# The edge list of a graph network's third layer: its search moved under the first attention and the neighbours' mean, its counting beside experts three to seven

## The chip, the cores and the metric

The kernel runs on one core of a Trainium2 chip. The metric is the device time of one launch in microseconds (us): the time before is 2432.49 us, the median of three runs (2429.66 to 2437.47). Engines are called as the profile calls them: PE multiplies matrices, DVE, ACT and POOL work on elements, SP issues most transfers.

## What is computed

The model has four layers over a graph of 2,708 nodes with 256 features each. Every layer normalises its input, mixes over the graph and adds, then normalises again, applies a feed-forward part and adds. Only the parts that this change touches are cut out here:

```python
# layer 0, over the graph: attention with weights exp(cosine) where adj > 0
x = x + _L0_gnn_ref(_layernorm(x), adj, ...)
# layer 1, over the graph: mean of the neighbours, projected
x1 = a @ x / deg
return concatenate([x1, x]) @ weight + bias
# layer 1, feed-forward: two of eight experts for each node
h = gelu(xf @ W1[e] + b1[e]);  out = out + w_dense[:, e] * (h @ W2[e] + b2[e])
# layer 2, over the graph: attention with leaky scores, softmax, elu
attention = softmax(where(adj > 0, leaky(wh1 + wh2.T), NEG_BIG));  elu(attention @ wh)
# layer 2, feed-forward: a router that reads a list of 1,048,576 edges
src, dst = edge_index;  e = leaky(a_src[src] + a_dst[dst]);  segment_max, segment_sum over dst
```

The edge list does not depend on any layer's result. Its nodes are drawn from 65,536 numbers and only those with a destination below 2,708 matter, so the kernel first searches the list for the edges that count and then counts them by destination. That work is needed only by the feed-forward part of layer 2.

## The kernel before

The queues of the five engines are ordered ahead of the run by a planner: of the instructions that are ready by its own costs it takes the one that was written earliest. `tc.issue_after(ins)` adds one condition: what is written in its block on the engine of `ins` comes behind `ins` on that engine. Instructions of the block on other engines are not bound by it. Functions that contain `yield` are generators; one `next` writes one step.

**First attention** (`fast_l0_gnn`). The 2,708 targets are cut into six chunks of 512 (the last has 148), the sources into 22 tiles of 128. For each pair of chunk and tile, `scores` loads a tile `aj` of the adjacency (SP, six buffers), multiplies keys and queries (L1791, PE), takes the exponential (L1815, ACT) and masks it (L1816, DVE). Two pairs later, `sums` multiplies the weights with the values (L1842, PE). At a chunk's end `finish` copies the four accumulators (L1862) and finishes the rows.

**Neighbours' mean** (`fast_l1_gnn`). For each of the same chunks in the order 0, 1, 5, 2, 3, 4 and for each tile, SP loads `aj` (ten buffers), ACT checks it (L2470), DVE casts it to `at` (L2495, ten buffers) and PE adds up (L2501). Beside it the router of the experts is computed by another generator, `after`.

**Experts** (`fast_l1_ffn`). For each of eight experts, POOL gathers 768 rows by index (`xe`, L2979), PE turns them (`xt_ps`, L3268) and multiplies them with both weight matrices (`h_ps`, L3282; `y_ps`, L3299), DVE adds the bias and scales (`ys`, L3307 and L3308), POOL adds the rows to `acc` in memory (L3311). `x` is read back from `acc` by `load_x` (L71) after the last expert's additions.

**The edge list** (`Edges`). `search` runs over eight chunks of 128 x 1,024 edges. Each is loaded by two transfers of 512 KB (L2592, L2594), turned into keys by five DVE instructions (L2597 to L2603), and its largest keys are taken out in nine rounds, eight at a time, by MAX8 and MATCH_REPLACE8 (L2608, L2609); a reduction (L2612) checks that nothing is left. `count` has a set-up on DVE (splitting the keys, taking out the rare edges, ranking them, with 32 products on PE, L2732), and then 18 count steps: each compares 32 keys with all node numbers (L2773: `oh` with 4,096 and `ol` with 704 elements to a partition) and adds up 32 products on PE (L2780).

In this version all of the search is written behind the experts: one step (a whole chunk) or more behind the last `ys` of each, by the numbers (1, 1, 2, 1, 2, 1, 3, 2). The third step of expert six is the whole set-up, the other four of experts six and seven are count steps. The other 14 count steps are written in the **second attention** (`fast_gat` with one head), one behind every fifth tile's weights (L3500, DVE; the sums are L3576, PE). The search waits for the router by a scalar, `route.start`, that enters its first instruction.

Of the kernel before, what the change touches and what calls it, by code (L numbers as in the profile page):

```python
# [8 lines left out]
F32 = mybir.dt.float32  # L9
# [1678 lines left out]
def fast_l0_gnn(k, adjT, wqkT, pool_):  # L1688
# [6 lines left out]
    with ExitStack() as ctx:  # L1695
# [88 lines left out]
        def scores(g, j):  # L1784
# [29 lines left out]
            for p, n, r, aj in todo:  # L1814
                nc.scalar.activation(PT[p, :n], s[p, :n], AF.Exp, scale=r)  # L1815
                nc.vector.scalar_tensor_tensor(  # L1816
                    PT[p, :n], aj[p, :n], 0.0, PT[p, :n], ALU.is_gt, ALU.mult
                )
            return PT

        last = {}
# [67 lines left out]
        for i in range(len(todo) + 2):  # L1889
            if i < len(todo):  # L1890
                ahead.append(scores(*todo[i]))
            for _ in range(2 if i < NT else 1):
                next(side, None)
            if i > 1:
# [7 lines left out]
        for _ in side:  # L1902
            pass
# [502 lines left out]
def fast_l1_gnn(k, adjT, weight, bias, order, after):  # L2406
# [6 lines left out]
    with ExitStack() as ctx:  # L2413
# [44 lines left out]
        tmp = ctx.enter_context(tc.tile_pool(name="a1o", bufs=4))  # L2458
# [26 lines left out]
        for i, g in enumerate(order):  # L2485
# [4 lines left out]
            for j in range(NT - 1):  # L2490
# [4 lines left out]
                nc.vector.tensor_copy(at[:, :cs], aj[:, :cs])  # L2495
# [48 lines left out]
            if i < len(order) - 1:  # L2544
                side = after(c0, cs, i, psum)

# [12 lines left out]
class Edges:  # L2559
# [12 lines left out]

    def __init__(self, k, w, pool):
# [9 lines left out]
    def search(self, n):  # L2583

        nc, tc = self.k.nc, self.k.tc
        L = self.L
        with tc.tile_pool(name="et", bufs=2) as tmp:
            ed = self.w["edge_index"].rearrange("s (p c) -> s p c", p=128)
            for c in range(CHEDGE):
# [5 lines left out]
                a = tmp.tile([128, CE], F32, name="a")  # L2595
                key = tmp.tile([128, CE], F32, name="key")
                nc.vector.tensor_scalar(a, si, 0.0, n, ALU.is_lt, ALU.mult)  # L2597
                nc.vector.scalar_tensor_tensor(a, si, 1.0, a, ALU.add, ALU.add)
                nc.vector.tensor_scalar(a, a, 1.0, float(N), ALU.max, ALU.min)
                nc.vector.scalar_tensor_tensor(  # L2600
                    key, di, float(1 << SHIFT), a, ALU.mult, ALU.add
# [3 lines left out]
                )  # L2605
                for r in range(RA):
# [4 lines left out]
                    )  # L2611
                nc.vector.tensor_reduce(self.left[:, c : c + 1], key, AX.X, ALU.max)  # L2612
                yield

    def count(self):
        nc, tc = self.k.nc, self.k.tc
        with tc.tile_pool(name="ep", bufs=1, side="right") as pp, tc.tile_pool(
# [28 lines left out]

            O = pp.tile([128, OA], F32, name="O")
# [25 lines left out]
            nc.vector.tensor_scalar(before, ioi, pc, None, ALU.is_gt)  # L2673
            rp = bank[:, : 5 * OW]
# [49 lines left out]
            for i in range(4):  # L2724
# [5 lines left out]
                )  # L2730
            for c in range(OA):
# [25 lines left out]

            nc.vector.tensor_scalar(hi, hi, 1.0, None, ALU.add)
            nc.vector.scalar_tensor_tensor(
                hi, sr, float(N - 1), hi, ALU.is_equal, ALU.mult  # L2760
            )
            nc.vector.tensor_scalar(hi, hi, -1.0, None, ALU.add)
            hib = pp.tile([128, LW], BF16, name="hib")
            lob = pp.tile([128, LW], BF16, name="lob")
            nc.vector.tensor_copy(hib, hi)
            nc.vector.tensor_copy(lob, lo)
# [92 lines left out]
class Route:  # L2859
# [14 lines left out]
    def __init__(self, k, ctx, w, most):  # L2874
# [13 lines left out]
        self.start = keep.tile([128, 1], F32, name="start")  # L2888
# [322 lines left out]
    def slots(self):  # L3211
# [6 lines left out]
        v.tensor_scalar(self.start, idf[:, 0:1], 0.0, float(N), ALU.mult, ALU.add)  # L3218
# [6 lines left out]
def fast_l1_ffn(k, side, route, rest):  # L3225

# [7 lines left out]
    with ExitStack() as ctx:  # L3234
# [119 lines left out]
        side = iter(side(route.start))  # L3354
        nxt = [one, half(0, 1)]
        run(first)
        for e in range(E):
# [13 lines left out]
            with tc.issue_after(now[-1].last.ins):  # L3371
                for _ in range((1, 1, 2, 1, 2, 1, 3, 2)[e]):
                    next(side)
        k.load_x(lambda r: acc[1 + r.start : 1 + r.stop], lambda ld: wait_for(ld, adds[E - 1]))


def fast_gat(k, adjT, W, a, H, elu, col, side, parts=CHUNKS, after=None):
# [10 lines left out]
    with ExitStack() as ctx:  # L3388
# [173 lines left out]
        for i, (c0, cs) in enumerate(parts):  # L3562
            if H == 1:
# [3 lines left out]
                for j in range(NT - 1):  # L3567
                    PT = weights(c0, cs, j, 0, adjacency(c0, cs, j))
                    if j % 5 == 4:
                        with tc.issue_after(made[0].ins):  # L3570
                            next(side, None)
# [898 lines left out]
def model(tc, I, out):  # L4470
# [4 lines left out]
    with tc.tile_pool(name="flags", bufs=1) as fp:  # L4475
# [4 lines left out]
        with ExitStack() as ctx:  # L4480
            k = Fast(ctx, tc, I["x"], bad, adjT)
            with ExitStack() as c0:
                pooling = Pooling(k, part(I, "L0_ffn_"), c0)
                fast_l0_gnn(k, adjT, I["L0_gnn_WqkT"], pooling)
# [108 lines left out]
```

## Time and profile before

| | |
|---|---|
| median of three runs | 2432.49 us |
| the profiled execution's own time | 2434.38 us |
| its span | 2432.6 us |
| granted clock of PE | 0.953 |
| PE busy | 2263.4 us (93%) |
| DVE busy | 1534.7 us (63%) |
| ACT busy | 666.4 us (27%) |
| POOL busy | 435.0 us (18%) |
| MAX8 and MATCH_REPLACE8, L2608 and L2609 | 72 each, 1225 and 1215 ns |
| count comparisons, L2773 | 18 of 4,466 ns and 18 of 930 ns |

The stages lie in this order in the profiled execution, by the first and last products of each: first attention 31.5 to 362 us, its feed-forward part to 557, projections of the mean to 610, neighbours' mean to 791, experts 797 to 1164.4, projections of the second attention from 1198.5, second attention 1235.1 to 1455.6, then the rest, which the change does not touch.

A row of a timeline gives start, length, engine, line, operation and tiles, and in brackets how long the engine was idle before it and what released it. PE's row of a group of products begins with the first and ends with the last of them. PE products of 32-bit data are recorded twice each.

### The profile page before, as it was taken

To read this page: it belongs to the slowest core of one execution; us is meant where nothing else is said; L and a number is where in the kernel's file an instruction comes from. 1 tells how busy PE (TensorE), PEld (TensorE's weight loads), DVE (VectorE), ACT (ScalarE), POOL (GpSimd) and SP (SyncE) were. 2 spreads that over 40 slices of the span, in tenths; PEclk is the share of its full clock that TensorE was granted. 3 is DMA by queue.
4 is the path that set the end of the run, shared out by engine and by line. 5 is a ranking of instruction groups with operands and counts; after the bars stand their busy time and mean duration, and the time that the engine had idled before them with its cause. 6 is when DMAs were issued, how large, how long until landed. Compare 5 with 4: busy or idle time off the path is not lost. (4 is left out here: it accounts for less than half of the span.)

```text
span 2432.6 us, 31798 instructions
## 1 busy us (share of the span) xinstructions
PE 2263.4 (93%) x11620; PEld 1512.2 (62%) x11620; DVE 1534.7 (63%) x3402; ACT 666.4 (27%) x1347; POOL 435.0 (18%) x496
## 2 busy tenths in 40 slices
PE   7999999988999899999599999999889999968997
PEld 4777765677878667767478877666653333325664
DVE  7544338555445378899779863142579999863544
ACT  6433333214663332231210013232321111111121
POOL 3000003004000333413350002520030000002321
PEclk9999999879999999999799997999899999978999
DMA  4233322200774344423244523000024444315440
GB/s 144 66 99 100 96 57 77 74 1 11 222 217 123 111 128 116 115 51 56 67 132 131 160 72 58 21 1 1 10 71 116 114 113 113 93 44 172 122 128 15
DMA packets 158572, 220.00 MB, mean 90 GB/s; under 512 B 30911, under 2 KB 94115, under 8 KB 158404
## 3 DMA queue, kind: packets, MB, share of 16 engines
q1 hardware_dynamic: 126096, 179.84, 25.4%
q0 software_dynamic: 15488, 24.04, 4.6%
q10 hardware_dynamic: 16820, 13.95, 1.8%
q8 instruction: 96, 1.57, 0.3%
q14 instruction: 72, 0.59, 0.1%
HBM read 193.49 MB, written 24.82 MB: 90 GB/s over the span
## 5 line engine op out<-in xcount | busy, mean ns | idle before, releaser
L3500 DVE SCALAR_TENSOR_TENSOR PT<-Rr,Q,aj 128x512 f32<-128x512 f32 (+3 forms) x630 | 403.2, 702 | 39.3 <-PE acc_ps L3576 26.9
L3651 PE MATMUL acc_ps<-PT,V 128*64 128x512 f32 (+4 forms) x2016 | 328.5, 549 | 0.4 <-ACT Rr L101 0.4
L3651 PEld LDWEIGHTS acc_ps<-PT,V 128*64 128x64 f32 (+1 forms) x2016 | 95.2, 122 | 210.2 <-issue 154.6
L1842 PE MATMUL acc_ps<-fa,PT 128*128 128x257 f32 x882 | 214.1, 382 | 0.5 <-DVE PT L1816 0.5
L1842 PEld LDWEIGHTS acc_ps<-fa,PT 128*128 128x128 f32 x882 | 164.6, 190 | 63.7 <-issue 41.0
L3576 PE MATMUL acc_ps<-V,PT 128*128 128x257 f32 x882 | 200.5, 385 | 2.6 <-DVE hp L3606 1.5
L3576 PEld LDWEIGHTS acc_ps<-V,PT 128*128 128x128 f32 x882 | 165.9, 191 | 31.4 <-issue 3.3
L3282 PE MATMUL h_ps<-xT,w1t 128*128 128x384 f32 x512 | 174.4, 499 | 4.5 <-ACT xT L3273 4.5
L3299 PE MATMUL y_ps<-w2t,hT 128*128 128x256 f32 x768 | 171.0, 382 | 2.7 <-DVE ys L3307 2.7
L1816 DVE SCALAR_TENSOR_TENSOR PT<-aj,PT 128x512 f32<-128x512 int32 (+1 forms) x126 | 79.8, 640 | 147.4 <-ACT PT L1815 147.3
L3299 PEld LDWEIGHTS y_ps<-w2t,hT 128*128 128x128 f32 x768 | 146.2, 192 | 25.3 <-DVE ys L3307 3.9
L2501 PE MATMUL acc_ps<-V,at 128*128 128x257 bf16 x1323 | 158.0, 278 | 3.6 <-DVE at L2495 3.6
L2501 PEld LDWEIGHTS <-at 128*128 128x128 bf16 x1323 | 130.0, 100 | 26.4 <-issue 4.9
L3282 PEld LDWEIGHTS h_ps<-xT,w1t 128*128 128x128 f32 x512 | 97.7, 194 | 73.3 <-ACT xT L3273 8.1
L1815 ACT ACTIVATE PT<-s_ps,rq 128x512 f32<-128x512 f32 (+1 forms) x126 | 79.3, 636 | 168.3 <-PE s_ps L1791 167.1
L3311 POOL DMA_INDIRECT acc<-ys,ids x48 | 86.2, 1796 | 216.3 <-DVE ys L3308 175.2
L1791 PE MATMUL s_ps<-KT,QT 128*128 128x512 f32 (+1 forms) x252 | 116.4, 546 | 1.1 <-POOL KT L1770 0.9
L3997 PE MATMUL y_ps<-w2t,hT 128*128 128x256 f32 (+1 forms) x528 | 117.2, 379 | 0.0
L3984 PE MATMUL h_ps<-fT,w1t 128*128 128x512 f32 (+1 forms) x288 | 115.6, 551 | 0.5 <-ACT hT L3991 0.4
L4420 PE MATMUL y_ps<-w2t,hT 128*128 128x256 f32 (+1 forms) x512 | 112.8, 379 | 0.0
L3997 PEld LDWEIGHTS y_ps<-w2t,hT 128*128 128x128 f32 (+1 forms) x528 | 97.7, 186 | 22.3 <-issue 8.2
L3289 ACT ACTIVATE hT<-h_ps,b1t 128x384 f32<-128x384 f32 x128 | 74.2, 580 | 113.4 <-PE h_ps L3282 112.7
(744 smaller groups left out, 3359.9 us busy)
## 6 DMA issues: line engine op xcount, KB each, us to landing
aj<-in_adjT SPq DMA_DIRECT2D x399, 256.0 KB
w1t<-in_L_ffn_W SPq DMA_DIRECT2D x8, 1024.0 KB
w2t<-in_L_ffn_W SPq DMA_DIRECT2D x8, 1024.0 KB
w1t<-in_L_ffn_w SPq DMA_DIRECT2D x8, 1024.0 KB
w2t<-in_L_ffn_w SPq DMA_DIRECT2D x8, 1024.0 KB
aj<-in_adjT SPq DMA_DIRECT2D x63, 74.0 KB
fd<-fa ACTq DMA_DIRECT2D x9, 512.0 KB
aj<-in_adjT SPq DMA_DIRECT2D x21, 202.0 KB
```

Source lines behind the costliest of these rows:

```text
L1791: nc.tensor.matmul(s[:, :cs], lhsT=QT[:, j * 128 : j * 128 + 128], rhs=KT[:, c0 : c0 + cs], start=True, stop=True,)
L1842: nc.tensor.matmul(ac, lhsT=PT[:, o : o + n], rhs=fa[:, j, :], start=j == 0, stop=False)
L2501: nc.tensor.matmul(ac[:, c:], lhsT=at[:, o : o + n], rhs=V[:, j, r], start=j == 0 and q == 0, stop=False, skip_group_check=True,)
L3282: nc.tensor.matmul(hp, lhsT=w1t[:, kk, m * 128 : (m + 1) * 128], rhs=self.xT[:, kk, :], start=(kk == 0), stop=(kk == 1),)
L3299: nc.tensor.matmul(y, lhsT=self.hT[:, m, i * 128 : (i + 1) * 128], rhs=w2t[:, m, :], start=(m == 0), stop=(m == M - 1),)
L3311: add = nc.gpsimd.indirect_dma_start(out=acc, out_offset=bass.IndirectOffsetOnAxis(ap=self.ids[:, i : i + 1], axis=0), in_=ys, in_offset=None,
L3500: return nc.vector.scalar_tensor_tensor(PT, R, Q, aj, ALU.max, ALU.mult)
L3576: nc.tensor.matmul(ac[:n], lhsT=PT[:, o : o + n], rhs=V[:, j, 0, :], start=(j == 0), stop=False,)
L3651: nc.tensor.matmul(w.pop("out"), **w)
L3984: nc.tensor.matmul(o[:, :cs], lhsT=w1t[:, kk, m * 128 : (m + 1) * 128], rhs=fT[:, kk, c0 : c0 + cs], start=(kk == 0), stop=(kk == 1),)
L3997: nc.tensor.matmul(y[:n], lhsT=hT[:, m, o : o + n], rhs=w2t[:, m, :], start=(m == 0), stop=(m == M - 1),)
L4420: nc.tensor.matmul(y[:n], lhsT=hT[:, m, o : o + n], rhs=w2t[:, m, :], start=(m == 0), stop=(m == M - 1),)
```

## The change

The list's tiles are made ahead of the first attention, and the search becomes a generator of small steps: one that loads, then eleven for each chunk (keys in two, each round of MAX8 and MATCH_REPLACE8 one; the reduction belongs to the last). The loads of the next chunk are written as soon as the keys of this one are made, into the same single buffers. Three searches share the eight chunks:

- chunks 0 to 3 in the first attention, one step behind the mask of every second pair, from the second target chunk on;
- chunks 4 and 5 in the neighbours' mean, one step behind every fourth cast of the first five chunks;
- chunks 6 and 7 behind experts 0 and 1 (12 and 11 steps). The set-up is cut into three steps, the first two behind expert 2, and the 18 count steps are spread behind experts 3 to 6 (four steps of which one is set-up, then 5, 5, 5), with one last copy behind expert 7.

The second attention gets no steps. The search no longer takes `route.start`, and the scratch pool of the mean has two buffers instead of four.

```diff
 def fast_l0_gnn(k, adjT, wqkT, pool_, other):
...
-                nc.vector.scalar_tensor_tensor(
+                made[0] = nc.vector.scalar_tensor_tensor(
                     PT[p, :n], aj[p, :n], 0.0, PT[p, :n], ALU.is_gt, ALU.mult
                 )
...
+            if i >= NT and i % 2:
+                with tc.issue_after(made[0].ins):
+                    next(other, None)
...
 def fast_l1_gnn(k, adjT, weight, bias, order, after, other):
...
-        tmp = ctx.enter_context(tc.tile_pool(name="a1o", bufs=4))
+        tmp = ctx.enter_context(tc.tile_pool(name="a1o", bufs=2))
...
-                nc.vector.tensor_copy(at[:, :cs], aj[:, :cs])
+                made = nc.vector.tensor_copy(at[:, :cs], aj[:, :cs])
+                if i < 5 and j % 4 == 1:
+                    with tc.issue_after(made.ins):
+                        next(other, None)
...
-    def search(self, n):
+    def search(self, chunks, side):
-        with tc.tile_pool(name="et", bufs=2) as tmp:
+        with tc.tile_pool(name="et", bufs=1, side=side) as tmp:
...
+            key = tmp.tile([128, CE], F32, name="key")
+            si, di = load(chunks[0])
+            yield
+            for c in chunks:
+                nc.vector.tensor_scalar(key, si, 0.0, float(N), ALU.is_lt, ALU.mult)
+                nc.vector.scalar_tensor_tensor(key, si, 1.0, key, ALU.add, ALU.add)
+                nc.vector.tensor_scalar(key, key, 1.0, float(N), ALU.max, ALU.min)
+                yield
                 nc.vector.scalar_tensor_tensor(
-                    key, di, float(1 << SHIFT), a, ALU.mult, ALU.add
+                    key, di, float(1 << SHIFT), key, ALU.mult, ALU.add
                 )
                 nc.vector.scalar_tensor_tensor(
                     key, key, float((N << SHIFT) + 1), key, ALU.is_lt, ALU.mult
                 )
+                if c != chunks[-1]:
+                    si, di = load(c + 1)
+                yield
                 for r in range(RA):
                     v = L[:, (c * RA + r) * 8 : (c * RA + r + 1) * 8]
                     nc.vector.max(v, key)
                     nc.vector.match_replace(
                         out=key, in_to_replace=v, in_values=key, imm_value=-1.0
                     )
+                    if r < RA - 1:
+                        yield
                 nc.vector.tensor_reduce(self.left[:, c : c + 1], key, AX.X, ALU.max)
                 yield
...
-        v.tensor_scalar(self.start, idf[:, 0:1], 0.0, float(N), ALU.mult, ALU.add)
...
+        steps_of = (12, 11, 2, 4, 5, 5, 5, 1)
...
             with tc.issue_after(now[-1].last.ins):
-                for _ in range((1, 1, 2, 1, 2, 1, 3, 2)[e]):
+                for _ in range(steps_of[e]):
                     next(side)
...
                 for j in range(NT - 1):
                     PT = weights(c0, cs, j, 0, adjacency(c0, cs, j))
-                    if j % 5 == 4:
-                        with tc.issue_after(made[0].ins):
-                            next(side, None)
...
+                    fast_l0_gnn(
+                        k, adjT, I["L0_gnn_WqkT"], pooling, edges.search(range(4), "right")
+                    )
...
+                        edges.search(range(4, 6), "left"),
...
+                    search = edges.search(range(6, CHEDGE), "right")
+                    fast_l1_ffn(k, chain(search, edges.count()), route, rest)
+                fast_gat(k, adjT, I["L2_gnn_W"], I["L2_gnn_a"], 1, True, 2, iter(()))
```

In `count`, two `yield`s are added in the set-up (ahead of the products that rank, and ahead of the 32 products L2732), and the nine lines that make `hib` and `lob`, the operands of L2773, move from the end of the set-up to its beginning.

## The prediction

> **What bounds the kernel now.** I read the busy times by stage first, then PE's timeline of the three stages that the edge list's work leaves or enters, then DVE, POOL and SP where a stage ends. Columns of the windows: length, then busy time and instructions of PE, PEld, DVE, ACT, POOL, then clock and DMA.
>
> ```profile
> 95.00:340.00 245.00, 245.00 (x1039) 177.42 (x1038) 96.60 (x254) 82.83 (x128) 0.00 (x0) 1.00 0.34 91
> 610.00:776.00 166.00, 162.37 (x1446) 134.53 (x1447) 77.34 (x262) 102.28 (x279) 1.23 (x3) 0.97 0.66 202
> 797.00:1164.40 367.40, 356.31 (x1412) 258.80 (x1413) 292.95 (x468) 92.49 (x167) 135.34 (x96) 0.98 0.37 94
> 1164.40:1198.50 34.10, 5.51 (x160) 5.30 (x159) 22.81 (x51) 2.32 (x4) 11.81 (x11) 0.55 0.43 109
> 1235.10:1455.60 220.50, 216.34 (x1415) 180.87 (x1415) 189.81 (x286) 12.76 (x28) 26.69 (x27) 0.99 0.44 129
> ```
>
> These are the first attention, the neighbours' mean, the experts, the gap behind them, and the attention behind (the second). PE sets the pace in all but the gap. DVE has room in the first two (39% and 47%), little in the experts (80%) and the second attention (86%).
>
> ```profile
> 1235.12 8.04 PE L3576 MATMUL acc_ps<-V,PT 128*128 128x257 f32 x36 [0.64 <-DMA aj<-in_adjT]
> 1244.80 0.95 PE L2780 MATMUL edge_ps<-ol,oh 128*128 128x22 bf16 x32 [1.64 <-DVE ol L2773]
> ...
> 1282.39 6.31 PE L3576 MATMUL acc_ps<-V,PT 128*128 128x257 f32 x28 [1.17 <-DVE hp L3606]
> ...
> 1323.84 6.31 PE L3576 MATMUL acc_ps<-V,PT 128*128 128x257 f32 x28 [0.38 <-DVE hp L3606]
> ...
> 1365.23 6.60 PE L3576 MATMUL acc_ps<-V,PT 128*128 128x257 f32 x28 [0.33 <-DVE rd L3602]
> ...
> 1403.68 37.05 PE L3576 MATMUL acc_ps<-V,PT 128*128 128x257 f32 x168
> 1441.30 2.00 PE L3576 MATMUL acc_ps<-V,PT 128*128 128x257 f32 x8
> ```
>
> Second attention, one line near each chunk's start: chunks with 4, 4, 4, 2 and 0 count steps take 47.3, 41.5, 41.4, 38.4 and 37.6 us.
>
> ```profile
> 896.10 0.82 PE L3268 MATMUL xt_ps<-ident,xe 128*128 128x128 f32 x6
> ...
> 939.50 0.82 PE L3268 MATMUL xt_ps<-ident,xe 128*128 128x128 f32 x6
> ...
> 1027.38 0.82 PE L3268 MATMUL xt_ps<-ident,xe 128*128 128x128 f32 x6
> ...
> 1086.22 32.98 PE L3299 MATMUL y_ps<-w2t,hT 128*128 128x256 f32 x144 [2.41 <-DVE ys L3307]
> 1119.03 0.82 PE L3268 MATMUL xt_ps<-ident,xe 128*128 128x128 f32 x6
> ...
> 1154.63 9.74 PE L3299 MATMUL y_ps<-w2t,hT 128*128 128x256 f32 x44
> ```
>
> Experts: expert 2 takes 43.4 us, undisturbed. Experts 3 and 4 take 87.9, 5 and 6 take 91.7, and expert 7, up to its last product at 1164.4, takes 45.3.
>
> ```profile
> 1157.37 5.42 POOL L3311 DMA_INDIRECT acc<-ys,ids  x1 [0.30 <-DVE rt L2697]
> ...
> 1171.09 4.43 DVE L2773 TENSOR_TENSOR oh<-io,lob 128x4096 bf16<-128x4096 bf16 x1
> 1171.55 5.39 POOL L3311 DMA_INDIRECT acc<-ys,ids  x1 [0.30 <-issue]
> ...
> 1179.16 0.93 SPq L71 DMA_DIRECT2D x<-acc  x2
> ```
>
> The gap: the expert's rows wait on DVE for the set-up, the last addition starts 7.2 us after the last product, is stretched by a count comparison from its usual 1.59 to 5.39 us, and only then are rows read back. PE waits until 1198.5.
>
> **The change, part by part.** Its stages by one profiled execution: 2434.4 us by its own time, of which the span is 2432.6. The median of the runs shown is 2432.5, 1.9 below.
>
> *Second attention: 14 counts leave.* Four chunks at 37.6 instead of 47.3, 41.5, 41.4 and 38.4 save 18.2; I keep 1 us back for the first chunk, where POOL still scales V beside DVE's products. **-17.** Nothing new comes up behind: without counts DVE needs some 21 x 0.70 = 15 us of 37.6, and chunk 4 shows transfers keeping up.
>
> *Experts: six of eight search chunks leave.* A chunk costs DVE about 29.5 us: five key operations 5.1 (0.76 to 1.23 each), nine rounds of MAX8 and MATCH_REPLACE at 2.58 (from MAX8 to MAX8), a reduction of 1.2. Six are 177 us. What that backlog costs PE: experts 3 to 7 took 87.9 + 91.7 + 45.3 = 224.9 against 5 x 43.4 = 217.0. **-8.**
>
> *The gap.* With one step (a copy of 0.18 us) left for expert 7, its last ys should follow the last product in some 0.9 us, POOL start its addition 0.3 later and need 1.6: 2.8, where it was 12.5 (1176.9). The read-back hangs on this. **-10.** Behind it SP's order remains: the weights for the next projection sit among chained x loads, and DVE waits 9.1 us for them; I leave that.
>
> *Experts: 18 counts and the rank products enter.* PE pays: with its overlap a count takes 1266.24 - 1265.43 = 0.81 us, so 18 are 14.6, and the 32 rank products take 1.6. **+16.** Fourteen of the counts are those that the second attention sheds; four and the rank products lay in the gap before, where PE had nothing else. DVE has room: a count is 4.42 + 0.88 = 5.3 us, five are 26.5 of 43 per expert, beside 6 x 0.77 for ys; three ys/y buffers cover 4.4 us of waiting (a y takes 3.4). PE is in order: if its count products stand ahead of DVE's comparison, it waits. In the second attention's chunks 1 to 3, with DVE full, PE never waited before a count; in chunk 0 1.64 and 0.53. Bounds -2 (counts filling PE's 0.3 us gaps) and +9 (0.5 each); I take **+2**.
>
> Two rules bear on this step. A bf16 comparison of 4,096 elements takes 4.42 us here; the Trainium skill (VectorE: DVE Perf Modes, the perf-mode tier table) lists bf16 tensor_tensor at 2x, 1.22 us for 2,048, so an estimate of 2.3. By it five counts would be 16 us and nearly free; the trace decides for 4.42. The second speaks against the change: the Trainium skill (SBUF — State Buffer, Who interferes with whom) says that a DVE instruction with two SBUF inputs and a GpSimd instruction that reads SBUF exclude each other for their whole length. The rows agree as far as they go: the additions of 5.42 and 5.39, and a gather of 7.91 at 942.9 beside key operations. By the rule POOL's six gathers (1.02), six additions (1.59) and 12 x 0.30 between, 19.3 us, plus 26.5 locked make 45.8 in an expert of 47: full. By the trace POOL waits 22.9 to 47.5 us at a stretch for ys, so there is slack: I take 0, up to +6 if gathers come late. In the first attention it costs nothing: POOL has no instruction there.
>
> *First attention: four chunks enter (8 loads, 44 DVE steps).* DVE goes from 96.6 to some 215 of 245. A mask starts every 2.59 us and leaves 1.90 free; a 2.58 round behind every second one delays the next by up to 0.7. The mask done at 202.84 is used at 206.41: 3.6 us of slack, so the steady part costs 0. At four chunk ends DVE also copies accumulators and finishes rows; there up to 2.5 us each may show. 0 to 10, I take **+2**: PE can bring forward a score product.
>
> *Neighbours' mean: two chunks enter (4 loads, 22 steps).* DVE from 77 to 136 of 166; casts run ten tiles ahead of PE, which hides a round. Not hidden: accumulators freed at five chunk ends (up to 1.2 each), and 1 MB of edges on SP at 610 to 630, where the transfers are full (385 GB/s): 2.7 us in front of tiles. 0 to 8, I take **+2**.
>
> *Other queues.* SP: one buffer instead of two, so a load waits for the chunk before; tiles queue behind it. Before, these loads held SP for 13.2 + 11.1 us in all, and adjacency tiles are six (15.5 us) or ten ahead: 0, or some 3 us per load if that lead is gone. POOL: two iotas (0.34) and four rank multiplications (1.13 each) move from expert 7 to expert 2: 0. The removed `start`, one small DVE instruction, only held the search behind the slots: 0. Two instead of four scratch buffers in the mean: their writers are in order on ACT or DVE: 0. The list's tiles opened earlier only occupy memory: 0.
>
> Sum: -17 - 8 - 10 + 16 + 2 + 2 + 2 = **-13**: 2421.4 on the profiled time, 2419.5 on the median; I say 2420.
>
> **Rivals.**
> *Cover used up.* The first attention and the mean take their upper ends or near (+7 and +5 instead of +2 each), the rest holds: -5, 2428. For: DVE at 88% and 82%, 11.6 of 15 us busy at a chunk end already. Against: 3.6 us and ten tiles of slack.
> *Slower: PE stands before counts.* The queue order is fixed by the planner's costs; with five counts back to back and less than 5.3 us of products between, PE waits for DVE 18 times in the stage it bounds. The two last counts in the gap waited 4.9 and 4.2 us with nothing in between. If the planner takes the comparison for half its length, some 2.65 us each: 48 instead of 2, so +33, 2466. It decides from (13 + 2)/18 = 0.8 us a count. Against: counts were placed without a wait in three chunks.
> *A larger gain.* The weights for the projection move ahead of the x loads on SP, or no cover costs anything: -6 to -13 more, about 2410. For: DVE's 9.1 us wait is an accident of order. Against: nothing in the diff touches it.
> *It doesn't do what it says:* steps left for the second attention. Experts: 1 + 2 x 11 + 22 = 45 steps, and 12 + 11 + 2 + 4 + 5 + 5 + 5 + 1 = 45; first attention 45 within 56 places, mean 23 within 25. Excluded.
>
> **How the numbers follow.** -13 as worked out 0.64, larger gain 0.15, cover used up 0.12, PE before counts 0.07, and 0.02 for a smaller slowdown. 0.3% (7.3 us) is about what a measurement of this kernel can tell from no change. Faster by more: nearly all of the first two: 0.78. Same: cover used up and an edge of the first: 0.14. Slower: 0.08. Range: below, the larger gain; above, cover used up plus late gathers: 2408 to 2432.
>
> **What would show it.** Second attention: no L2780, five chunks of 37 to 38 us each. Last product to read-back of x: 5 us instead of 14.8. Experts 4 to 7: some 47 us each, with edge_ps products between those of h and y and no waits before them. First attention: MAX8 and MATCH_REPLACE in DVE's pauses between masks, PE still busy throughout. I would be wrong if PE waits for ol or oh in the experts, if xt waits for xe, if PE idles at chunk ends of the first attention, or if the gap stays near 34 us.

## The result, and the profile after

The changed kernel takes 2416.55 us, the median of ten runs (2413.13 to 2419.71), against 2429.83 for the kernel before in ten runs on the same chip: a ratio of 0.9943, with a 95% interval of 0.993 to 0.9956. That is 13.3 us less, more than the 0.3% (7.3 us) that the prediction took as the least that can be told from no change. The predicted time was 2420, the predicted sum -13.

The profiled execution has a span of 2411.6 us, 21.0 below that of before. More than the medians' 13.3 lies between these two because the profiled execution of before was 4.6 above its median and this one 3.2 below. Lines of the changed kernel are numbered a little differently (L1792 scores, L1817 mask, L1844 sums, L2502 and L2511 the mean's cast and sums, L2798 and L2805 count, L3003 gather, L3290 `xt`, L3304 `h`, L3321 `y`, L3333 addition, L3598 the second attention's sums).

First the windows of the five stages, placed where they lie now. The columns are length, then busy time and instructions of PE, PEld, DVE, ACT and POOL, then clock and DMA.

```profile
95.00:345.00 250.00, 248.76 (x1047) 177.83 (x1046) 199.28 (x386) 84.13 (x131) 0.00 (x0) 1.00 0.36 102
617.10:801.60 184.50, 175.57 (x1596) 144.80 (x1596) 135.58 (x352) 100.64 (x279) 3.54 (x5) 0.98 0.61 194
804.40:1182.10 377.70, 370.58 (x2026) 272.97 (x2026) 225.46 (x333) 94.86 (x170) 173.07 (x105) 0.99 0.33 77
1182.10:1195.80 13.70, 0.02 (x1) 0.00 (x0) 5.42 (x24) 2.61 (x5) 2.17 (x6) 0.61 0.64 175
1237.10:1439.80 202.70, 202.41 (x968) 168.52 (x968) 120.62 (x252) 13.51 (x29) 17.50 (x22) 1.00 0.50 141
```

DVE went up in the first two (to 80% and 73%), down in the experts (60%) and the second attention (60%). PE still sets the pace in four of them, and the gap is 13.7 us where it was 34.1. The mean, though, has nine us in which PE is not busy (184.5 against 175.6), where the whole stage had 3.8 before.

PE in the second attention, its first chunk and the start of the next:

```profile
1237.17 36.66 PE L3598 MATMUL acc_ps<-V,PT 128*128 128x257 f32 x168 [0.57 <-ACT Rr L101]
1273.76 0.72 PE L3619 MATMUL acc_ps<-Vt,PT 32*128 32x257 f32 x8
1274.41 5.82 PE L3598 MATMUL acc_ps<-V,PT 128*128 128x257 f32 x24
```

One row of 168 products, with no count and no wait in it: 37.2 us, and the next four chunks take 37.6 each.

PE in expert 6, one row of each kind (`xt`, a count, `h`, the last count, `y`, the next expert's `xt`):

```profile
1086.12 0.82 PE L3290 MATMUL xt_ps<-ident,xe 128*128 128x128 f32 x6
...
1092.50 0.95 PE L2805 MATMUL edge_ps<-ol,oh 128*128 128x22 bf16 x32
1093.31 4.76 PE L3304 MATMUL h_ps<-xT,w1t 128*128 128x384 f32 x14
...
1114.15 0.96 PE L2805 MATMUL edge_ps<-ol,oh 128*128 128x22 bf16 x32
1114.96 19.24 PE L3321 MATMUL y_ps<-w2t,hT 128*128 128x256 f32 x88
1134.04 0.82 PE L3290 MATMUL xt_ps<-ident,xe 128*128 128x128 f32 x6
```

The expert takes 47.9 us. The next `h` starts 0.81 us after a count's first product, none of these rows has a wait in brackets, and 88 products of `y` follow undisturbed.

The gap, from the timelines of POOL, SP, DVE (two rows) and PE (two rows):

```profile
1183.24 1.54 POOL L3333 DMA_INDIRECT acc<-ys,ids  x1 [1.91 <-DVE cnt L2813]
...
1186.92 0.93 SPq L71 DMA_DIRECT2D x<-acc  x2
...
1191.08 0.75 DVE L1640 BATCH_NORM_STATS2 ln_st<-x 128x6 f32<-128x256 f32 x2 [8.02 <-DMA x<-acc]
...
1198.49 0.42 DVE L3439 TENSOR_TENSOR pr<-w,ar 128x256 f32<-128x256 f32 x1 [0.78 <-DMA ar<-in_L_gnn_a]
...
1195.85 3.37 PE L1610 MATMUL ft_ps<-ident,fa 128*128 128x128 f32 x16 [13.73 <-DVE fa L1654]
1202.60 7.75 PE L3455 MATMUL v_ps<-w,fT 128*128 128x258 f32 x27 [3.39 <-DVE w L3445]
```

The last product ends at 1182.1. The last addition takes 1.54 us and the read-back starts 4.8 us behind the last product (14.8 before). The second thing to see is DVE's order: it takes the first rows of `x` as they land, at 1191.1, and the product with `ar` only at 1198.5. Before, the same product stood in front of the rows:

```profile
1190.69 0.42 DVE L3414 TENSOR_TENSOR pr<-w,ar 128x256 f32<-128x256 f32 x1 [9.08 <-DMA ar<-in_L_gnn_a]
1191.08 0.43 DVE L1640 BATCH_NORM_STATS2 ln_st<-x 128x6 f32<-128x256 f32 x1
```

There the read-back was issued at 1179.2 and the first statistics came 11.9 us later. Now they come 4.2 us after it.

PE's first `ft_ps` follows the last product by 13.7 us instead of 34.2, which is 20.4 less. Of these, 4.7 are lost again before the second attention starts, 3.4 of them in the wait for `w` in the last row of PE above. So 15.7 are left.

### The profile page after: what moved, and what is told of

The parts are those of the page before. It is cut to its first block, busy times and chain, and to the rows that moved or that the text cites. A ratio compares the mean times of both kernels' runs of the same rounds, so it can differ in the third digit from the quotient of the medians.

```text
span 2411.6 us, 31812 instructions
## 1 busy us (share of the span) xinstructions
PE 2255.9 (94%) x11620; PEld 1500.7 (62%) x11620; DVE 1533.7 (64%) x3401; ACT 666.4 (28%) x1347; POOL 454.6 (19%) x496
## 5 line engine op out<-in xcount | busy, mean ns | idle before, releaser
L3525 DVE SCALAR_TENSOR_TENSOR PT<-Rr,Q,aj 128x512 f32<-128x512 f32 (+3 forms) x630 | 408.4, 703 | 86.9 <-PE acc_ps L3598 75.1
L1844 PE MATMUL acc_ps<-fa,PT 128*128 128x257 f32 x882 | 215.4, 383 | 1.2 <-DVE out L1864 1.2
L1844 PEld LDWEIGHTS acc_ps<-fa,PT 128*128 128x128 f32 x882 | 163.9, 190 | 66.5 <-issue 33.8
L3598 PE MATMUL acc_ps<-V,PT 128*128 128x257 f32 x882 | 195.4, 382 | 0.8 <-ACT Rr L101 0.6
L3598 PEld LDWEIGHTS acc_ps<-V,PT 128*128 128x128 f32 x882 | 165.8, 190 | 29.8 <-PE acc_ps L3598 2.3
L3304 PE MATMUL h_ps<-xT,w1t 128*128 128x384 f32 x512 | 176.5, 498 | 3.5 <-ACT xT L3295 3.5
L3321 PE MATMUL y_ps<-w2t,hT 128*128 128x256 f32 x768 | 169.8, 380 | 0.0
L2511 PE MATMUL acc_ps<-V,at 128*128 128x257 bf16 x1323 | 156.7, 277 | 10.1 <-DVE at L2502 8.2
L3321 PEld LDWEIGHTS y_ps<-w2t,hT 128*128 128x128 f32 x768 | 144.9, 190 | 21.1
L2511 PEld LDWEIGHTS <-at 128*128 128x128 bf16 x1323 | 128.9, 99 | 32.9 <-DVE at L2502 5.7
L3304 PEld LDWEIGHTS h_ps<-xT,w1t 128*128 128x128 f32 x512 | 95.9, 193 | 68.0 <-ACT xT L3295 8.5
L3333 POOL DMA_INDIRECT acc<-ys,ids x48 | 92.0, 1916 | 155.1 <-DVE ys L3330 144.7
L1792 PE MATMUL s_ps<-KT,QT 128*128 128x512 f32 (+1 forms) x252 | 116.2, 548 | 2.5 <-ACT PT L1816 1.6
L3003 POOL DMA_INDIRECT xe<-fd,idg x48 | 79.7, 1661 | 194.7 <-DVE early_f L3034 180.3
L1817 DVE SCALAR_TENSOR_TENSOR PT<-aj,PT 128x512 f32<-128x512 int32 (+1 forms) x126 | 79.2, 633 | 57.9 <-ACT PT L1816 57.5
```

The costliest lines, as they stand in the source:

```text
L1792: nc.tensor.matmul(s[:, :cs], lhsT=QT[:, j * 128 : j * 128 + 128], rhs=KT[:, c0 : c0 + cs], start=True, stop=True,)
L1844: nc.tensor.matmul(ac, lhsT=PT[:, o : o + n], rhs=fa[:, j, :], start=j == 0, stop=False)
L2511: nc.tensor.matmul(ac[:, c:], lhsT=at[:, o : o + n], rhs=V[:, j, r], start=j == 0 and q == 0, stop=False, skip_group_check=True,)
L3304: nc.tensor.matmul(hp, lhsT=w1t[:, kk, m * 128 : (m + 1) * 128], rhs=self.xT[:, kk, :], start=(kk == 0), stop=(kk == 1),)
L3321: nc.tensor.matmul(y, lhsT=self.hT[:, m, i * 128 : (i + 1) * 128], rhs=w2t[:, m, :], start=(m == 0), stop=(m == M - 1),)
L3525: return nc.vector.scalar_tensor_tensor(PT, R, Q, aj, ALU.max, ALU.mult)
```

## Where the time went, stage by stage

Distances between the same products in both traces (us). The last column is a second profile of the changed kernel (the run e11 below), since single executions differ.

| stage | before | changed | difference | difference, second profile |
|---|---|---|---|---|
| start of the span to the first attention's last products | 363.4 | 369.4 | +6.0 | +5.7 |
| layer 0's feed-forward part and projections | 247.4 | 247.7 | +0.3 | -1.3 |
| neighbours' mean, first to last product | 180.1 | 184.0 | +3.9 | +6.3 |
| experts, first xt to last y | 369.9 | 377.7 | +7.8 | +9.4 |
| last y to the second attention's first product | 70.7 | 55.1 | -15.7 | -15.8 |
| second attention | 221.1 | 202.6 | -18.5 | -16.8 |
| start of layer 2's feed-forward part, first ft_ps to first y_ps | 41.3 | 36.4 | -4.9 | -2.1 |
| all else | 938.7 | 938.7 | 0.0 | -0.5 |

The columns add up to -21.1 and -15.1, the spans differ by 21.0 and 15.0. What is to be explained: the cover cost ten to twelve us instead of four, the gap gave 15.7 instead of 10, and the start of layer 2 was not in the prediction at all.

## Experiments

Ratios are to the kernel before, timed on the same chip, with their 95% intervals.

### What the first attention pays (e1)

```diff
-  edges.search(range(4), "right")
+  edges.blank(range(4))          # fills the list's part with zeros
```

> The changed kernel with the search of chunks 0 to 3 left out of the first attention (their part of the list is filled with zeros, so the router of layer 2 reads other counts). Theory, from the two traces: those 44 steps delay the end of the first attention by 6.0 us (last tail product 362.7 before, 368.8 after), about 1.1 at each of the chunk ends behind them; then this kernel takes 2416.6 - 6 = 2410.5, a ratio to the kernel before of 0.992, and its last tail product lies at 362.7. By the prediction's step of +2 it would take 2414.5. Rival, full cover: the 6 us are a difference of the executions and not of the search; then no change against the changed kernel, 2416.5, and a last tail product near 368.8.

Its time, 2485.03 us (ratio 1.0224, 1.0207 to 1.0241), can't be read: with other counts layer 2 and what follows does other work, and the span after layer 2's first y_ps is 1003.7 us instead of 931. Up to there it is the same program but for the search. The next-to-last group of tail products starts at 362.70, to 0.04 us where it was before; in the changed kernel it is 368.76. So the 6 us are the search's, and the rival of full cover is out. The chunks of 512 targets behind the first take 56.7 us each without the search (the last of them 55.5). In the changed kernel three of them take 1.0 more, which makes 3.2 with the first. The other 2.8 lie in the last chunk, of 148 targets: 26.45 us instead of 23.62 between the tail groups at its two ends.

How a chunk end loses its 1.0 is seen in DVE's timeline of the changed kernel, with PE's behind it:

```profile
287.24 1.22 DVE L2629 MAX8 L<-key 128x8 f32<-128x1024 f32 x1
288.38 0.41 DVE L1864 COPY out<-acc_ps 128x257 f32<-128x257 f32 x1
...
288.84 0.70 PE L1844 MATMUL acc_ps<-fa,PT 128*128 128x257 f32 x2 [0.40 <-DVE out L1864]
```

The accumulator's copy stands behind a MAX8, and PE, which needs the accumulator for the next chunk, waits for the copy. PE's record shows 0.40 of the 1.0; the rest lies in products that are spaced wider.

The loss in the last chunk begins at a chunk end too, the fourth. Of the search only the last round and the reduction lie in this chunk, at its start. DVE in the changed kernel and, second, in e1, from the second mask of the chunk to the third:

```profile
342.83 0.31 DVE L1817 SCALAR_TENSOR_TENSOR PT<-aj,PT 128x148 f32<-128x148 int32 x1 [1.19 <-ACT PT L1816]
343.06 1.22 DVE L2629 MAX8 L<-key 128x8 f32<-128x1024 f32 x1
344.20 0.41 DVE L1864 COPY out<-acc_ps 128x257 f32<-128x257 f32 x1
...
346.05 1.21 DVE L2635 TENSOR_REDUCE left<-key 128x1 f32<-128x1024 f32 x1
347.18 0.30 DVE L1817 SCALAR_TENSOR_TENSOR PT<-aj,PT 128x148 f32<-128x148 int32 x1
```

```profile
339.60 0.31 DVE L1817 SCALAR_TENSOR_TENSOR PT<-aj,PT 128x148 f32<-128x148 int32 x1 [1.67 <-ACT PT L1816]
...
342.06 0.30 DVE L1817 SCALAR_TENSOR_TENSOR PT<-aj,PT 128x148 f32<-128x148 int32 x1
```

The third mask comes 4.35 us behind the second with the search and 2.46 without it. How these 1.9 us become 2.8 by the end of the chunk was not taken apart.

### What the mean pays (e2)

```diff
-  edges.search(range(4, 6), "left")
+  edges.blank(range(4, 6))
```

> The changed kernel with the search of chunks 4 and 5 left out of the neighbours' mean (zeros in their place, so the router of layer 2 reads other counts). Theory: the search costs the mean some 4 us (its last products at 801.1 instead of 790.8, of which 6.4 were there at its start), 3.4 of them in one wait of PE for at at 623, behind 1 MB of edges that SP issued at 614.9: 2412.6 and no such wait. By the prediction's step of +2: 2414.5. Rival: the adjacency loads themselves cause the wait, as they start 6.4 us later; then it stays, and the time is 2416.

2408.98 us, ratio 0.9908 (0.9893 to 0.9923); here the work after layer 2's start has its usual length (931.4), so the time can be read. That is 7.6 us below the changed kernel's median, or 8.5 by the ratios, more than the 4 expected. The mean takes 177.5 us from its first to its last product. In all profiles without its search it takes 177.5 to 180.1 (four of them), and in seven with the changed kernel's steps there, 184.0 to 186.7. So the first profile of the changed kernel shows the cheapest of seven, and the usual price is 7. PE's first row in the mean, here and (three rows) in the changed kernel:

```profile
615.63 29.91 PE L2511 MATMUL acc_ps<-V,at 128*128 128x257 bf16 x252 [3.65 <-DVE at L2502]
```

```profile
617.13 2.83 PE L2511 MATMUL acc_ps<-V,at 128*128 128x257 bf16 x24 [3.47 <-DVE at L2502]
623.39 28.18 PE L2511 MATMUL acc_ps<-V,at 128*128 128x257 bf16 x228 [3.43 <-DVE at L2502]
654.94 6.08 PE L2511 MATMUL acc_ps<-V,at 128*128 128x257 bf16 x53 [0.92 <-DVE x L2549]
```

Without the search the first chunk is one row of 252 products. With it there is a second wait, for the cast of a tile that came late, and at the next chunk's start one for the rows `x`, which free the accumulators.

### What the counts cost PE (e3)

```diff
             for s0 in range(0, LW, HB):
-                oh = hot.tile([128, HB, 128], BF16, name="oh")
...
-                    nc.vector.tensor_tensor(
...
-                    nc.tensor.matmul(
...
                 yield
-            nc.vector.tensor_copy(self.cnt, cp)
+            nc.vector.memset(self.cnt, 0.0)
```

> The changed kernel without the 18 count steps (comparisons and products left out, the counts set to zero; the set-up with its ranks stays). Theory: in the experts PE pays for the products alone, 0.81 us a count, and waits nowhere: experts 4 to 7 go from 46.2, 47.9, 47.9 and 48.1 back to 43.4 each, and the time falls by 18 x 0.81 = 14.6 to 17 us, to some 2401. Rival, a wait hidden in the lengths: DVE or POOL held up by the comparisons costs more than the products, then by 20 or more. Rival, counts in PE's gaps: by less than 10.

Again the time (2476.21, ratio 1.0188, 1.0174 to 1.0202) is that of other work behind layer 2's start. The experts can be read. They take 363.3 us, against 377.7 and 379.3 in the two profiles of the changed kernel: 14.4 to 16.0 for 18 counts, 0.80 to 0.89 each. The first rows of `xt` of three experts, with no count between them:

```profile
1038.63 0.82 PE L3272 MATMUL xt_ps<-ident,xe 128*128 128x128 f32 x6
...
1082.08 0.82 PE L3272 MATMUL xt_ps<-ident,xe 128*128 128x128 f32 x6
...
1125.54 0.82 PE L3272 MATMUL xt_ps<-ident,xe 128*128 128x128 f32 x6
```

43.45 us each. So PE pays for the products and for next to nothing else: both rivals are out. This run also tests the rule on DVE and GpSimd. The gathers (min, median and max in ns), in the changed kernel and, second, without the comparisons:

```profile
L3003 POOL DMA_INDIRECT xe<-fd,idg x48: 999/1034/4939, 798.3 to 1102.9; - x48
```

```profile
L2985 POOL DMA_INDIRECT xe<-fd,idg x48: 999/1025/1441, 799.5 to 1087.9; - x48
```

With the comparisons gone, no gather takes more than 1.44 us. With them gathers take up to 4.94. Expert 6 of the changed kernel shows one beside a comparison (a row of DVE, then one of POOL):

```profile
1092.19 4.42 DVE L2798 TENSOR_TENSOR oh<-io,lob 128x4096 bf16<-128x4096 bf16 x1
1093.20 4.36 POOL L3003 DMA_INDIRECT xe<-fd,idg  x1 [0.30 <-issue]
```

The gather ends 1.0 us after the comparison, about its usual length of 1.03: POOL is held while the comparison runs, as the Trainium skill (SBUF — State Buffer, Who interferes with whom) has it for a DVE instruction with two SBUF inputs. It cost PE nothing here: the three long gathers of expert 6 end at 1107.8, and their rows are first needed at 1134.0.

### The counts back in the second attention (e4)

```diff
-  steps_of = (12, 11, 2, 4, 5, 5, 5, 1)
+  steps_of = (12, 11, 2, 5, 0, 0, 0, 0)
...
+                    if j % 5 == 4:
+                        with tc.issue_after(made[0].ins):
+                            next(side, None)
```

> The changed kernel with 14 of the 18 counts put back into the second attention, one behind every fifth tile; the other four stay beside expert five, so the gap stays free. Theory: in the second attention they cost 18.2 us as in the kernel before (chunks of 47.3, 41.5, 41.4, 38.4 against 37.6), in the experts they save 14 x 0.81 = 11.3 or a little more: 5 to 7 us slower than the changed kernel, some 2423, still faster than before. Rival, the move of the counts is the whole gain: 2430 as before. Rival, it is worth nothing and the gap and the search are all: 2417.

2424.06 us, ratio 0.9974 (0.9964 to 0.9984): 7 us slower than the changed kernel, at the theory's upper end. (The four counts that stay lie beside expert 4, as the experts are numbered here from 0.) The second attention takes 220.8 us, 16.6 to 18.2 more than in the two profiles of the changed kernel; the experts take 365.6, 12.1 to 13.7 less. So a count costs 1.2 to 1.3 us in the second attention and some 0.9 beside the experts. The move of the 14 counts alone is worth three to six us by the stages and seven by the medians: about half of the 13 at most.

### Only the gap (e5)

The kernel before, with nothing of the edge list behind its last expert:

```diff
-  for _ in range((1, 1, 2, 1, 2, 1, 3, 2)[e]):
+  for _ in range((1, 1, 2, 1, 2, 1, 1, 0)[e]):
```

> The kernel before with one thing changed: nothing of the edge list is written behind the last expert. The set-up comes one expert earlier, and all 18 counts are in the second attention instead of 14. Theory, by the traces: the last expert's products to the read-back of x shrink from 14.8 to 5 us (-10), and the read-back to the first product of the next projection from 19.4 to 9 or to the projection itself by 6, because DVE no longer stands for ar ahead of the first rows; four more counts in the second attention cost about 1.0 each (+4) to 2.4 each (+10). So -6 to -12: 2418 to 2424. Rival, the prediction's account, in which the wait for ar stays: -10 + 4 to 10, so 0 to -6: 2424 to 2430.

2419.47 us, ratio 0.9959 (0.9941 to 0.9977): 11.3 us by the medians, 10 by the ratio. The set-up does not change its place in the program: in the kernel before it is the first of expert 6's three steps, not the third, and it stays that here. Four counts leave the experts. In the trace the set-up's 32 products run beside expert 7, at 1151.0, where they ran 3.3 us behind the last y; expert 7 takes 49.5 us instead of 45.3. The last y to the second attention's first product takes 55.1 us as in the changed kernel (70.7 before), and 18 counts in the second attention make it 3.8 longer. DVE and PE in its gap:

```profile
1171.90 0.75 DVE L1640 BATCH_NORM_STATS2 ln_st<-x 128x6 f32<-128x256 f32 x2 [8.09 <-DMA x<-acc]
...
1176.72 3.65 PE L1610 MATMUL ft_ps<-ident,fa 128*128 128x128 f32 x16 [13.76 <-DVE fa L1654]
```

DVE takes the rows first here too. So the whole 15.7 of the gap comes from what stood behind the last expert, and its second part, about 5.7, comes with the first: the planner, which orders by its own costs, now puts the product with `ar` behind the first rows instead of in front. Which of its costs decides that was not tried. The prediction's account, in which that wait stays, is out.

This run also weighs the rest of the change. Against 13.3 us for the whole, the free gap alone gives 10 to 11. The search under the two stages and the counts beside the experts together add some 2 to 4, and the intervals (0.9941 to 0.9977 here, 0.993 to 0.9956 for the changed kernel) don't tell that from nothing.

### Steps away from the chunk ends (e6)

```diff
-            if i >= NT and i % 2:
+            if i >= NT and i % 2 and i % NT > 3:
```

> The changed kernel, with the search's steps in the first attention kept away from the ends of the target chunks: nine steps in a chunk instead of eleven, none in the first four pairs. Theory: the cost there is the accumulators' copies held up by rounds of MAX8 and MATCH_REPLACE8; without that some 4 of the 6 us come back: 2412.5, and no wait of PE for L1864's out. Rival, the cost is spread over all pairs: no gain, 2416.5, or a loss because the search ends later.

2424.61 us, ratio 0.9976 (0.9966 to 0.9987): 8 us slower than the changed kernel. Yet the half that it was made for came true. The chunks of 512 take 56.7 us each (the last of them 55.5), as without a search, though six or seven rounds lie in each; and no wait for `out` is left. The loss is the one that the rival names, a search that ends later. What was taken from the ends went into the last chunk: nine rounds lie in it, where the changed kernel has one, and it takes 34.2 us instead of 26.5. There DVE's timeline reads:

```profile
359.03 1.22 DVE L2629 MAX8 L<-key 128x8 f32<-128x1024 f32 x1
360.17 0.29 DVE L1817 SCALAR_TENSOR_TENSOR PT<-aj,PT 128x148 f32<-128x148 int32 x1
360.38 0.08 DVE L2630 MATCH_VALUE_LOAD key<-L,key 128x8 f32 x1
360.45 1.21 DVE L2630 MATCH_REPLACE8 key<-L,key 128x1024 f32<-128x1024 f32 x1
361.58 0.30 DVE L1817 SCALAR_TENSOR_TENSOR PT<-aj,PT 128x148 f32<-128x148 int32 x1
361.80 1.22 DVE L2629 MAX8 L<-key 128x8 f32<-128x1024 f32 x1
```

A pair of this chunk needs PE for about 1.1 us (23.6 us for 22 tiles); masks come every 1.4 us, because each stands behind a MAX8 or a MATCH_REPLACE8, which cost the same beside 148 targets as beside 512. The tail group that started at 362.7 starts at 372.2, and the mean 6.6 us later than in the first profile of the changed kernel. The steps are counted in tiles, but a tile of this chunk takes less than half as long as one of 512 targets (1.1 us against 2.59).

### The mean's edge loads later (e7)

```diff
-                if i < 5 and j % 4 == 1:
+                if 0 < i < 5 and j % 3 == 1:
```

> The changed kernel, with the mean's part of the search begun at its second target chunk and written behind every third cast instead of every fourth from the first chunk on. Theory: the 3.4 us that PE waits at 623 come from the edge loads among adjacency loads that run at full rate; later there is room, so the wait goes: 2413. Rival: the loads take the same 2.7 us from the adjacency wherever they lie, and the denser steps hold up casts: 2416.5 or more.

2415.47 us, ratio 0.9933 (0.9913 to 0.9953): no difference from the changed kernel that can be told. The wait at the start is gone, and the mean takes 185.5 us all the same, with its short chunk at 19.4 us between the tail groups at its ends instead of 16.6 (14.5 before). My theory, that the early edge loads are the main cost, fell. What is left is the steps on DVE, here in denser order; e9 below shows that their places set the price.

### The weights by another queue (e8)

```diff
+            q = nc.scalar if H == 1 else nc.sync
-            nc.sync.dma_start(w[:, :, :D], W.rearrange("(k p) c -> p k c", p=128))
+            q.dma_start(w[:, :, :D], W.rearrange("(k p) c -> p k c", p=128))
...
-                nc.sync.dma_start(
+                q.dma_start(
                     ar[:, s, :, :].rearrange("p h f -> p (h f)"), brow(a[s], D)
```

> The changed kernel, with the weights w and the vectors ar of the second attention's projection loaded through ACT's queue instead of SP's, where they stand between the chained loads of x. Theory: PE's wait of 3.39 us for w ahead of the first v_ps goes: -2 to -4, 2413 to 2414.5. Rival: the 0.5 MB then shares the transfers with the rows of x, the first rows come as much later: no change, 2416.5.

2419.0 us, ratio 0.9948 (0.9928 to 0.9967): no gain. DVE and PE in the gap show why, and neither theory had it:

```profile
1196.78 0.43 DVE L3440 TENSOR_TENSOR pr<-w,ar 128x256 f32<-128x256 f32 x1 [10.74 <-DMA ar<-in_L_gnn_a]
...
1204.38 2.17 PE L1610 MATMUL ft_ps<-ident,fa 128*128 128x128 f32 x9 [19.29 <-DVE fa L1654]
```

With the loads on a queue that is free, the product with `ar` is again put ahead of the rows, and DVE stands for 10.7 us. PE's wait for `w` is gone, but its first ft_ps comes 19.3 us after the last y instead of 13.7. That is the order of before in the changed kernel, and it repeats the mechanism: DVE's order, not the order on SP, decides when the projection starts. Of the 5.6 us, 1.3 are left at the second attention's first product (56.3 us behind the last y), as the wait for `w` is saved.

### Versions from the findings, and the changed kernel again (e9, e10, e11)

```diff
-            if i >= NT and i % 2:
+            if i >= NT and i % 2 and i % NT > 3:
...
-  edges.search(range(4), "right")
+  edges.search(range(3), "right")
...
-                if i < 5 and j % 4 == 1:
+                if i in (0, 1, 3, 4) and j % 3 == 1 and j > 1:       # e9
-  steps_of = (12, 11, 2, 4, 5, 5, 5, 1)
+  steps_of = (12, 11, 11, 2, 4, 5, 5, 0)                           # e9
+  steps_of = (12, 11, 11, 11, 11, 4, 5, 0)                         # e10, no search in the mean
...
+                    if j % 5 == 4 and c0 > 0:
+                        with tc.issue_after(made[0].ins):
+                            next(side, None)
```

> A version built from the findings: three instead of four chunks of the search in the first attention, none of their steps in the first four pairs of a target chunk or in the short last chunk; two chunks in the mean, none of their steps at the start of a chunk or in the short one; three beside experts 1 to 3; thirteen counts beside experts 5 to 7 and five in the second attention from its second target chunk on; nothing behind the last expert. Theory (the cover costs 13 us in the changed kernel, at chunk ends and in the short chunks): the first attention gives back 6, the mean about 5; one more chunk beside the experts costs 1.3 and five counts in the second attention 1.0 instead of 0.85 each: some 9 to 10 faster than the changed kernel, 2407, ratio to before 0.9905. Rival, the cost is one of DVE's fill and goes where the steps go: 2416.

> As the version above in the first attention and the gap, but no search in the mean: five chunks beside experts 1 to 5, the set-up and one count beside expert 6, five counts beside expert 7, the other twelve in the second attention from its second target chunk on. Theory: first attention -6, mean -7, three more chunks beside the experts 1.3 each, twelve counts at 1.0 instead of 0.85: -7 to -8, some 2409, ratio 0.991. Rival, DVE is too full beside the experts (29.5 for a chunk and 9.2 for ys of 43.4) and falls behind as in the kernel before: an extra 5 to 8, 2416.

> The changed kernel itself once more, for a second profile and for times on the same chip as the two versions above. If the stages of the first profile are typical, the mean takes 184 us from its first to its last product and the start of layer 2's feed-forward part, from the first ft_ps to the first y_ps, 36.4. If they were that execution's luck, they take 185 to 186.5 and 39.1 as in the seven other profiles with the same work there.

| | us, median | ratio to before | first attention's tail group | mean | experts | second attention |
|---|---|---|---|---|---|---|
| e11, changed kernel | 2417.05 | 0.9950 (0.9936 to 0.9963) | 368.5 | 186.4 | 379.3 | 204.3 |
| e9 | 2408.38 | 0.9916 (0.9890 to 0.9943) | 363.0 | 180.7 | 373.7 | 209.5 |
| e10 | 2409.42 | 0.9923 (0.9897 to 0.9948) | 362.5 | 178.3 | 371.4 | 216.6 |

The lines marked e9 and e10 differ between the two, and the last three put the other counts into the second attention. Both land close to where they were expected, about 8 us below the changed kernel. Intervals overlap by a little (0.9936 to 0.9943 for e9, to 0.9948 for e10), so that they beat the changed kernel rests on the stages as well as on the medians. The first attention pays nothing for three chunks with no steps at chunk ends and none in the short chunk. The mean pays two instead of seven for its two chunks when they avoid the same places. e10 shows that DVE beside the experts carries five chunks without falling behind, one beside each of the experts 1 to 5. PE's first `xt` of two of them:

```profile
935.07 0.82 PE L3290 MATMUL xt_ps<-ident,xe 128*128 128x128 f32 x6
...
978.52 0.82 PE L3290 MATMUL xt_ps<-ident,xe 128*128 128x128 f32 x6
```

These five experts take 43.4 or 43.5 us each, as expert 2 did in the kernel before, which also had one chunk beside it. So one chunk to an expert costs PE nothing. What is left to explain the 7.9 us that experts 3 to 7 cost too much in the kernel before is the two chunks behind each of experts 2 and 4, and the set-up. So five chunks could have stayed with the experts, spread evenly. The second profile of the changed kernel settles the first one's luck: 186.4 for the mean and 39.2 for the start of layer 2.

## Why the prediction was right, and where its steps were not

*Second attention, -17:* right in mechanism and size: -18.5 and -16.8 in two profiles, and 18.2 came back in e4.

*Experts, -8 + 16 + 2:* right. Eighteen counts cost 14.4 to 16.0 (e3). Without them the experts are 6.6 shorter than before, though the ranks that came in cost the 1.9 by which expert 3 is longer: about -8.5 for the six chunks that left. By e10 it was more their uneven places than their number that cost PE time. The +2 for waits did not show. The rival in which PE stands before counts is out: no wait before a count, against 0.8 us each from which it would have decided.

*POOL, 0 with up to +6:* right at 0. POOL was held beside comparisons, and there was slack. The estimate of 2.3 us for a comparison says little about this one: both its operands are broadcasts (`to_broadcast`), which the estimate did not consider, and one of plain operands was not run.

*The gap, -10:* the read-back came as worked out, 4.8 us after the last product where 5 was predicted. The step that failed is the sentence "Behind it SP's order remains ... I leave that". SP's order did remain. DVE's did not, and that gave 5.7 more (10.4 at the first `ft_ps`, of which 4.7 were lost again), which e5 shows to come with the free gap. The rival of a larger gain named DVE's wait as an accident of order and had the wrong queue; its against, that nothing in the diff touches it, was the error: an order made by costs is touched by whatever changes when the engine is free.

*First attention, +2:* mis-sized, 6, inside its own range of 0 to 10. "The steady part costs 0" held: away from chunk ends, six or seven rounds in a chunk of 512 cost nothing (e6). The term for the four chunk ends was too small: 1.0 at each of three, and 2.8 behind the fourth, where the tiles are short. So this term failed, not the one for the steady part.

*Mean, +2:* mis-sized, about 7 (3.9 in the profile shown), inside its range of 0 to 8. Moving the early loads, one of the two named costs, brought nothing back, with the steps in denser order (e7). The short chunk added 2.1 and was not named.

So the parts had the right signs, but that the total of -13 fits the medians so well is luck: two errors nearly cancel, 9 us too little for the cover and 6 too little for the gap. Of the 21.0 between the two profiles, the start of layer 2 is 4.9 that no edit aims at; 2.8 of it lie between two executions of the changed kernel, and the other 2.1 stay open. The first profile's cheap mean is some 2 more.

## What to carry to other kernels

Price background work by the shortest tile that it can land behind, not by the usual one: a step of fixed length that is free beside 512 columns holds up the engine beside 148 (e6), and at a chunk's end it stands in front of the copy that frees an accumulator. Spread it evenly: one chunk to an expert was free (e10). When an engine's queue is ordered by a cost model, look behind the wait that you remove for instructions that were ordered around it; here they were worth half as much again. And try the cheapest edit alone: keeping the last expert's end clear took one line (e5) and gave most of the gain.

## What the runs showed of the hardware

PE's first products in layer 2's feed-forward part, in the kernel before, and its granted clock there (the last column but two of the windows) in the kernel before, the changed kernel, and the changed kernel's second profile:

```profile
1460.28 3.77 PE L1610 MATMUL ft_ps<-ident,fa 128*128 128x128 f32 x16 [4.09 <-issue]
```

```profile
1465.00:1490.00 25.00, 23.57 (x111) 22.28 (x111) 10.21 (x43) 8.67 (x18) 0.00 (x0) 0.50 0.19 61
```

```profile
1448.00:1458.00 10.00, 9.57 (x72) 9.06 (x71) 8.18 (x36) 5.94 (x12) 0.00 (x0) 0.83 0.01 2
```

```profile
1457.00:1477.00 20.00, 17.20 (x80) 15.65 (x79) 7.12 (x29) 6.65 (x14) 0.00 (x0) 0.50 0.35 113
```

After an idle stretch of 4.1 us the clock is at half and, before, stays there for over 25 us while PE is recorded busy for 23.6 of 25; the products of 24 columns take 214 ns each at that clock and 128 where it is 0.88 (32 of them in 6.86 and 4.11 us). The Trainium skill (TensorE: Matmul & The Clock Gate, Part 1: The HAM clock gate) gives about 3.4 us of activity as the price of warming up; in this stage the half clock lasted several times that, and for how long differed between two executions of one program (39.2 and 36.4 us for the stage). What ends it was not tried.
